# Fetching a part of an embedding lookup row by row from two other DMA issuers

## The chip, the cores and the metric

The kernel runs on one core of a Trainium2 chip. A core has TensorE (PE, matrix products and transposes), VectorE (DVE), ScalarE (ACT), GpSimd (POOL) and SyncE (SP), which run their own instruction streams and meet at semaphores, and 16 DMA engines that move data for all of them. SyncE, ScalarE and GpSimd can issue DMAs. The metric is the device time of one execution in microseconds; before the change it is 11255.83 us, the median of 3 runs (11247.95 to 11278.97).

## What is computed

A recommendation model with attention over 69 id fields. For each of 16384 samples, one label row and 69 field rows of 96 float32 numbers (384 bytes) are looked up in a table of 100001 rows:

```python
u = emb[batch_user]                       # (16384, 69, 96)
ql = emb[batch_label[:, 0]]               # (16384, 96)
q = broadcast(ql over the fields)
z = concatenate([q, u, q - u, q * u], -1)
h = dice(z @ W1 + b1, a1)                 # 384 -> 64
att = (h @ W2 + b2) @ W3 + b3             # -> one number for each field
pre = where(batch_user < 100000, u * att, 0)
pooled = einsum('gf,bfe->bge', window, pre)       # 10 groups of fields
x = concatenate([pooled, ql], -1)                 # 11 * 96
h = dice(bn(x @ Wf1 + bf1)); h = dice(bn(h @ Wf2 + bf2)); out = h @ Wf3 + bf3
```

`dice(x, a)` is `(a * (1 - p) + p) * x` with `p` the sigmoid of the scaled `x`. The lookups are 16384 x 70 rows, 440 MB.

## The kernel before

The batch is cut into 32 blocks of 512 samples. A block has 69 chunks of 512 rows, two of them a "pair" (1104 pairs in all), and a chunk has 4 tiles of 128 rows. A tile is fetched with one indirect DMA, issued by GpSimd, which reads 128 ids from memory:

```python
def gather(table, dst, index):
    nc.gpsimd.indirect_dma_start(out=dst, out_offset=None, in_=table,
        in_offset=bass.IndirectOffsetOnAxis(ap=index, axis=0))          # L257

def head_gather(n):                       # the labels of block n: 4 tiles
    q = bpool.tile([P, NQ, E], F32, tag="q", name=f"q{n}")
    for k in range(NQ):
        gather(emb, q[:, k, :], ids[n][:, NT + k : NT + k + 1])
    return q

def head_turn(n, q):                      # turned to 96 x 512
    pq = ps_x.tile([E, BLK], F32, tag="x", name=f"pq{n}")
    for k in range(NQ):
        nc.tensor.transpose(pq[:, k * P : (k + 1) * P], q[:, k, :], ident)
    nc.vector.tensor_copy(qTs[n % 2][0:E, 0:BLK], pq)
```

A pair is fetched, turned on TensorE, multiplied with the labels on VectorE and copied out of PSUM by ScalarE:

```python
def fetch(i, between=None):
    u = upool.tile([P, 8, E], F32, tag="u", name=f"u{i}")     # upool has 14 buffers
    ...
    for j in range(2):
        n, k = chunk(2 * i + j)
        ptr = ps_tr.tile([E, 512], F32, tag="tr", name=f"ptr{i}_{j}")   # 2 buffers
        for t in range(4):
            gather(rows, u[:, 4 * j + t, :], ids[n][:, 4 * k + t : 4 * k + t + 1])
            nc.tensor.transpose(ptr[:, t * P : (t + 1) * P], u[:, 4 * j + t, :], ident)   # L313
        ...   # VectorE: quT = ptr * labels (L316)
        nc.scalar.copy(uT[j][0:E], ptr)                                 # L325
```

Two steps later `hidden` multiplies with W1 (L338, L342) and forms the dice (ScalarE L344, L345; VectorE L346); then come the attention rows (`attend_rows`, L353) and their turning (`spread`, L370, L375), and eight steps after the fetch `pool` weighs the rows themselves, `acc <- rw, u` (L397). A `u` buffer is free again only after that. Each step `i` of the plan records, in this order:

```python
POOL_LAG = 8
...
at(i, pool_of(i - POOL_LAG)); ...; at(i, tails_of(i - 3)); ...; at(i, hidden_of(i - 2)); at(i, fetch_of(i))
...
for n in range(NBLK):
    first = n * NCH // 2                  # the block's first pair
    if n > 0:
        ...                               # every 4th block: load_ids
        at(first - 14, head_gather of n); at(first - 11, head_turn of n); at(first - 9, head_rows of n)
    ...                                   # the top layers of each block, spread over steps
```

Every engine executes its own instructions in the order in which they are recorded.

Of the kernel before, what the change touches and what calls it, by code (L numbers as in the profile page):

```python
# [32 lines left out]
F32 = mybir.dt.float32  # L33
I32 = mybir.dt.int32
# [4 lines left out]
P = 128  # L39
B, F, E, G = 16384, 69, 96, 10  # L40
ITEM_NUM = 100000
# [5 lines left out]
NBLK = B // BLK  # L47
# [4 lines left out]
NCH = NMAIN + NTAIL  # L52
NQ = BLK // P
NT = NCH * 4
# [5 lines left out]

POOL_LAG = 8

NIDS = 4

EARLY = 20
# [49 lines left out]
def rec_kernel(  # L115
    ctx: ExitStack,
    tc: tile.TileContext,
    idx0: bass.AP,
    idx: bass.AP,
    emb: bass.AP,  # L120
    rows: bass.AP,
    near: bass.AP,
# [3 lines left out]
    nc = tc.nc  # L126
# [4 lines left out]
    tpool = ctx.enter_context(tc.tile_pool(name="tpool", bufs=4))  # L131
    ypool = ctx.enter_context(tc.tile_pool(name="ypool", bufs=6))
    rpool = ctx.enter_context(tc.tile_pool(name="rpool", bufs=2))
    bpool = ctx.enter_context(tc.tile_pool(name="bpool", bufs=2))
    xpool = ctx.enter_context(tc.tile_pool(name="xpool", bufs=1))

    def by_field(ap):

        return ap.rearrange("e (s o) -> e s o", o=1).to_broadcast([ap.shape[0], NS, FM])

    ids = {0: const.tile([P, NCOL], I32, name="ids0")}
    nc.sync.dma_start(out=ids[0], in_=idx0)

    def load_ids(n):

        t = ipool.tile([P, NIDS, NCOL], I32, tag="ids", name=f"ids{n}")
        nc.sync.dma_start(out=t.rearrange("p b n -> p (b n)"), in_=idx[(n - 1) // NIDS])
        for k in range(NIDS):
            ids[n + k] = t[:, k, :]
# [7 lines left out]
    ident = const.tile([P, P], F32, name="ident")  # L157
# [26 lines left out]
    for i in range(2):  # L184
        t = const.tile([E + 1, BLK], F32, name=f"qT{i}")
# [70 lines left out]
    def gather(table, dst, index):  # L256
        nc.gpsimd.indirect_dma_start(  # L257
            out=dst,
            out_offset=None,
            in_=table,  # L260
            in_offset=bass.IndirectOffsetOnAxis(ap=index, axis=0),
        )

    def chunk(c):

        n, k = divmod(c, NCH)
        if n == NBLK - 1 and k >= EARLY:
            k = NMAIN + k - EARLY if k < EARLY + NTAIL else k - NTAIL
        return n, k

    def head_gather(n):

        q = bpool.tile([P, NQ, E], F32, tag="q", name=f"q{n}")
        for k in range(NQ):
            gather(emb, q[:, k, :], ids[n][:, NT + k : NT + k + 1])
        return q

    def head_turn(n, q):
        pq = ps_x.tile([E, BLK], F32, tag="x", name=f"pq{n}")
# [4 lines that stand above are left out]
    def head_rows(n):  # L284

        for h in range(2):
            pc = ps_x.tile([P, NMAIN // 8, H1], F32, tag="x", name=f"pc{n}_{h}")
            for k in range(NMAIN // 8):
                x = (h * NMAIN // 8 + k) * 4 * NS
                nc.tensor.matmul(pc[E:P, k, :], qTs[n % 2][:, x : x + 4 * NS], Cq, start=True, stop=True)  # L290
            nc.scalar.copy(As[n % 2][E:P, h * NMAIN // 8 : (h + 1) * NMAIN // 8, :], pc[E:P])
# [3 lines left out]
    def room(k):  # L295

        v = k % 4 if k < NMAIN else turns.index(min(turns))
        turns[v] += 1
        return uTs[v][turns[v] % len(uTs[v])]

    def fetch(i, between=None):

        u = upool.tile([P, 8, E], F32, tag="u", name=f"u{i}")
        uT = []
        quT = tpool.tile([E, 2, 512], F32, tag="quT", name=f"quT{i}")
        for j in range(2):
            if j == 1 and between:
                between()
            n, k = chunk(2 * i + j)
            ptr = ps_tr.tile([E, 512], F32, tag="tr", name=f"ptr{i}_{j}")  # L310
            for t in range(4):
                gather(rows, u[:, 4 * j + t, :], ids[n][:, 4 * k + t : 4 * k + t + 1])
                nc.tensor.transpose(ptr[:, t * P : (t + 1) * P], u[:, 4 * j + t, :], ident)  # L313
            q = qTs[n % 2][0:E]
            if k < NMAIN:
                nc.vector.tensor_tensor(  # L316
                    quT[:, j, :].rearrange("e (s f) -> e s f", f=FM),
                    ptr.rearrange("e (s f) -> e s f", f=FM),
                    by_field(q[:, k * NS : (k + 1) * NS]),
                    ALU.mult,  # L320
                )
            else:
                nc.vector.tensor_tensor(quT[:, j, :], ptr, q[:, 0:BLK], ALU.mult)
            uT.append(room(k))
            nc.scalar.copy(uT[j][0:E], ptr)  # L325
        return u, uT, quT

    def hidden(i, uT, quT):

# [57 lines left out]
    def pool(i):  # L387

        u, rw = us.pop(i), rws.pop(i)
        todo = [(j, *chunk(2 * i + j)) for j in range(2)]  # L390
        todo = [(j, n, k) for j, n, k in todo if k < NMAIN]
        if not todo:
            return
        pa = ps_acc.tile([E, 2, NS, G], F32, tag="acc", name=f"acc{i}")
        for j, n, k in todo:
            for t in range(4):
                nc.tensor.matmul(  # L397
                    pa[:, j, 2 * t : 2 * t + 2, :].rearrange("e n g -> e (n g)"),
                    u[:, 4 * j + t, :],
                    rw[:, t, j, :],  # L400
                    start=True,
                    stop=True,
                )
        if len(todo) == 2:
            _, n, k = todo[0]
            nc.vector.tensor_copy(  # L406
                pooled[n][:, :, k * NS : (k + 2) * NS].rearrange("e g s -> e s g"),
                pa.rearrange("e j s g -> e (j s) g"),
            )
        else:  # L410
            j, n, k = todo[0]
            nc.vector.tensor_copy(
                pooled[n][:, :, k * NS : (k + 1) * NS].rearrange("e g s -> e s g"), pa[:, j]
            )
# [43 lines left out]
    def store(n):  # L458

        p4 = ps_x.tile([n, P], F32, tag="x", name="p4")  # L460
        nc.tensor.transpose(p4, res[:, 0:n], ident)
        r = ypool.tile([P, 512], F32, tag="y", name="r")[0:n, 0:P]
        nc.vector.tensor_copy(r, p4)
        nc.sync.dma_start(out=out[0 : n * P].rearrange("(m p) o -> m (p o)", p=P), in_=r)
# [9 lines left out]
    pooled, pres, x1s, x2s, qs, us, hs, ys, bands, rws, p1s = ({} for _ in range(11))  # L474

    def top_steps(n, cols):


        def half(h, part):
            if n not in x1s:  # L480
                x1s[n] = xpool.tile([DH, 2, BLK], F32, tag="x1", name=f"x1_{n}")
            p1s[n] = top1(n, cols, h, part, p1s.get(n))

        steps = [lambda h=h, part=part: half(h, part) for h in range(2) for part in range(4)]
        steps.append(lambda: x2s.__setitem__(n, top2(n, cols)))
        if n * BLK + cols.stop < B:
            steps.append(lambda: top3(n, cols, x2s.pop(n)))
        else:
            steps.append(lambda: top3_last(x2s.pop(n)))
        return steps  # L490
# [7 lines left out]
    def pool_of(k):  # L498
        return lambda: pool(k)
# [28 lines left out]
    def at(step, *work):  # L528
        plan.setdefault(step, []).extend(work)
# [25 lines left out]
    for n in range(NBLK):  # L555
        first, end = n * NCH // 2, ((n + 1) * NCH - 1) // 2
        if n > 0:
            if n % NIDS == 1:
                at(first - 20, lambda n=n: load_ids(n))
            at(first - 14, lambda n=n: qs.__setitem__(n, head_gather(n)))  # L560
            at(first - 11, lambda n=n: head_turn(n, qs.pop(n)))
            at(first - 9, lambda n=n: head_rows(n))
        if n < NBLK - 2:
            for s, work in enumerate(top_steps(n, slice(0, BLK))):
                at(end + POOL_LAG + 4 + s, work)
        elif n == NBLK - 2:
            for s, work in enumerate(top_steps(n, slice(0, BLK))):
                at(end + POOL_LAG + s // 2, work)
# [10 lines left out]
    at(d, quarter[2][8], spread_of(c + 6, 2), quarter[2][9], quarter[3][0])  # L579
    at(d, pool_of(c + 6), pool_of(c + 7), lambda: store(B // P - 1), *quarter[3][1:])  # L580

    with tc.manual_schedule():
        qs[0] = head_gather(0)
        head_turn(0, qs.pop(0))
        head_rows(0)
        ones()
        for i in range(NPAIR + 1):
            for work in plan.pop(i, []):
                work()
    assert not plan  # L590


# [60 lines left out]
```

## Time and profile before

| | us |
|---|---|
| timed, median of 3 | 11255.83 |
| span of the profiled execution | 13170.6 |
| GpSimd busy in it | 8455.0 (8966 instructions) |
| TensorE busy in it | 8747.3 |
| ScalarE busy in it | 3167.1 |
| VectorE busy in it | 3029.0 |

The profiled execution is longer than the timed ones, so durations of single instructions and the spacing of undisturbed neighbours are read from it, and the total is taken from the timed runs. In the groups of the profile a row names the source line, engine, operation and operands, then the count, the busy time and the mean of one in ns, and the idle time of the engine just before such instructions with what ended most of it. "issue" means that the engine waited for nothing that the profile shows. A timeline row has the start in us, the duration, and in brackets the idle time before it. "SPq" and "ACTq" are the instruction streams that issue DMAs on SyncE and ScalarE. The DMA queues' part shows 286720 packets of the gathers, which take 16.0% of the 16 DMA engines' time.

### The profile page before, as it was taken

What the parts mean: (1) busy time and instruction counts of PE and PEld (TensorE: products, weight loads), DVE (VectorE), ACT (ScalarE), POOL (GpSimd) and SP (SyncE); (2) the same over time, 40 slices, a digit from 0 to 9 for tenths busy, and PEclk for the clock granted to TensorE, in tenths of its full rate; (3) what the DMA queues carried; (4) which work ended last, traced back from release to release, by engine and by line L of the source; (5) the groups of instructions that cost most, each with busy time, mean ns of one, the idle gap of its engine ahead of it and who ended that gap; (6) DMA issues with size and microseconds to landing.
All of it is one profiled execution on the core that took longest, in us unless ns stands there. A gap on an engine that the chain in (4) does not pass through costs nothing.

```text
span 13170.6 us, 108463 instructions
## 1 busy us (share of the span) xinstructions
PE 8747.3 (66%) x41797; PEld 4554.2 (35%) x41797; DVE 3029.0 (23%) x5325; ACT 3167.1 (24%) x4969; POOL 8455.0 (64%) x8966
## 2 busy tenths in 40 slices
PE   3666666667666676666766667666666666676667
PEld 2333333333333333333333333333333333333334
DVE  2222222222222222222222222222222222222222
ACT  1222222222222222222222222222222222222222
POOL 6666666666666666666666666666666666666664
PEclk6777777777777777767777777777777777777777
DMA  1111111111111111111111111111111111111111
GB/s 40 35 35 34 34 34 37 34 36 34 34 36 34 35 35 35 37 34 34 35 34 37 33 35 34 34 36 35 35 35 33 36 34 35 35 35 35 35 34 22
DMA packets 288946, 454.19 MB, mean 34 GB/s; under 512 B 143538, under 2 KB 143922, under 8 KB 288306
## 3 DMA queue, kind: packets, MB, share of 16 engines
q0 software_dynamic: 286720, 440.98, 16.0%
q8 instruction: 335, 5.49, 0.2%
q1 hardware_dynamic: 1570, 5.04, 0.1%
q14 instruction: 177, 1.45, 0.0%
q10 hardware_dynamic: 144, 1.24, 0.0%
HBM read 446.61 MB, written 0.07 MB: 34 GB/s over the span
## 4 chain that ended last, share of the span: by engine, by line
PE 54%; issue 20%; another core or an unknown queue 16%; POOL 4%; ACT 3%; DVE 3%; DMA 1%; DVEq 0%; POOLq 0%
PE acc L397 11%; PE ptr L313 9%; PE ph L338 9%; PE ph L342 8%; PE p L436 7%; PE prow L353 4%; POOL u L257 3%; PE patt L370 1%; DVE quT L316 1%; PE pa L362 1%; ACT uT L325 1%; ACT y L345 1%; PE ph L335 1%; PE pc L290 1%
## 5 line engine op out<-in xcount | busy, mean ns | idle before, releaser
L257 POOL DMA_INDIRECT u<-in_rows,ids x8832 | 8333.2, 944 | 4552.4 <-issue 2367.4
L397 PE MATMUL acc<-rw,u 128*96 128x20 f32 x16384 | 1922.1, 260 | 1844.3 <-issue 1436.2
L397 PEld LDWEIGHTS acc<-rw,u 128*96 128x96 f32 x16384 | 1911.1, 197 | 2083.9 <-issue 1613.1
L313 PE MATMUL ptr<-ident,u 128*96 128x128 f32 x8832 | 1594.5, 316 | 1395.4 <-issue 1099.1
L325 ACT COPY uT<-ptr 96x512 f32<-96x512 f32 x2208 | 1283.3, 581 | 3091.3 <-DVE quT L316 1905.9
L313 PEld LDWEIGHTS ptr<-ident,u 128*96 128x96 f32 x8832 | 1079.1, 143 | 2732.2 <-issue 2182.7
L344 ACT ACTIVATE y<-ph 128x512 f32<-128x512 f32 x1104 | 659.3, 597 | 5104.0 <-remote 2661.7
L342 PE MATMUL ph<-quT,wn 96*64 96x512 f32 x4416 | 1693.6, 744 | 165.9 <-issue 158.6
L346 DVE TENSOR_TENSOR y<-ph,y 128x512 f32<-128x512 f32 x1104 | 763.5, 692 | 4287.1 <-ACT y L345 2399.0
L338 PE MATMUL ph<-uT,A 128*64 128x512 f32 x4096 | 1631.8, 800 | 145.8 <-issue 142.8
L316 DVE TENSOR_TENSOR quT<-ptr,qT 96x512 f32<-96x512 f32 x2048 | 1337.6, 680 | 1419.3 <-remote 892.2
L406 DVE COPY pooled<-acc 96x160 f32<-96x160 f32 x1008 | 429.6, 426 | 3547.6 <-remote 2121.3
L345 ACT ACTIVATE y<-y,wn,na1c 128x512 f32<-128x512 f32 x1104 | 897.8, 813 | 36.7
L342 PEld LDWEIGHTS ph<-quT,wn 96*64 96x64 f32 x4416 | 449.0, 172 | 1201.8 <-issue 1199.3
L353 PE MATMUL prow<-y,v 128*32 128x512 f32 x2208 | 629.5, 787 | 254.1 <-issue 150.2
L436 PE MATMUL p<-pooled,wf 96*100 96x512 f32 (+1 forms) x1400 | 616.5, 583 | 0.0
L338 PEld LDWEIGHTS ph<-uT,A 128*64 128x64 f32 x4096 | 280.6, 162 | 683.7 <-issue 664.9
L355 ACT COPY row<-prow 128x512 f32<-128x512 f32 (+1 forms) x277 | 161.8, 584 | 1421.8 <-remote 878.8
L370 PE MATMUL patt<-ident,row 128*128 128x128 f32 x1108 | 241.2, 338 | 277.6 <-issue 203.7
L436 PE MATMUL p<-pre,V 96*100 96x512 f32 (+1 forms) x700 | 372.7, 665 | 40.6 <-issue 25.8
L436 PEld LDWEIGHTS p<-pooled,wf 96*100 96x100 f32 x1400 | 233.7, 179 | 291.7 <-issue 291.6
L375 DVE SCALAR_TENSOR_TENSOR rw<-patt,bb,wn 128x320 f32<-128x320 f32 x554 | 273.4, 534 | 142.2 <-remote 64.3
(66 smaller groups left out, 2139.8 us busy)
## 6 DMA issues: line engine op xcount, KB each, us to landing
u<-in_rows,ids POOLq DMA_INDIRECT x8832
ids<-in_idx SPq DMA_DIRECT2D x8, 560.0 KB
q<-in_emb,ids POOLq DMA_INDIRECT x128
wf<-in_far ACTq DMA_DIRECT2D x1, 1209.0 KB
wn<-in_near SPq DMA_DIRECT2D x1, 236.0 KB
ids<-in_idx SPq DMA_DIRECT2D x1, 140.0 KB
out<-r SPq DMA_DIRECT2D x1, 63.5 KB
out<-r SPq DMA_DIRECT2D x1, 0.5 KB
```

Of the source, the lines that this page charges most:

```text
L257: nc.gpsimd.indirect_dma_start(out=dst, out_offset=None, in_=table, in_offset=bass.IndirectOffsetOnAxis(ap=index, axis=0),)
L313: nc.tensor.transpose(ptr[:, t * P : (t + 1) * P], u[:, 4 * j + t, :], ident)
L316: nc.vector.tensor_tensor(quT[:, j, :].rearrange("e (s f) -> e s f", f=FM), ptr.rearrange("e (s f) -> e s f", f=FM), by_field(q[:, k * NS ...
L325: nc.scalar.copy(uT[j][0:E], ptr)
L338: nc.tensor.matmul(p, As[n % 2][:, k // 4, :], uT[j], start=True, stop=False)
L342: nc.tensor.matmul(p, Wp, quT[:, j, :], start=False, stop=True)
L344: nc.scalar.activation(y, ph, AF.Sigmoid, scale=S_DICE)
L345: nc.scalar.activation(y, y, AF.Identity, bias=a1c, scale=na1c)
L346: nc.vector.tensor_mul(y, ph, y)
L353: nc.tensor.matmul(pr[32 * k : 32 * (k + 1), :], v2, ys[b + k], start=True, stop=True)
L397: nc.tensor.matmul(pa[:, j, 2 * t : 2 * t + 2, :].rearrange("e n g -> e (n g)"), u[:, 4 * j + t, :], rw[:, t, j, :], start=True, stop=True,)
L436: nc.tensor.matmul(p1, w[:, h * DH : (h + 1) * DH], x, start=(k == 0), stop=(k == KTOP - 1))
```

## The change

GpSimd issues one indirect DMA for 128 rows. The change takes 7 of the 280 such DMAs of each block but the first away from GpSimd: the four tiles of label rows, and the first tile of the chunks 8, 24 and 40 (the tiles 32, 96 and 160, "solo"). Their rows are fetched one by one, each by a plain DMA of 384 bytes whose source address comes from a register: SyncE issues the first 96 rows of a tile, ScalarE the other 32. The ids come in a new input, `solo`, in the order of use, and are loaded into registers 24 (SyncE) or 8 (ScalarE) at a time. The aim is to relieve GpSimd of issue work.

```diff
+SOLO = [4 * 8, 4 * 24, 4 * 40]
+NROW = NQ + len(SOLO)                    # 7 tiles in a block
+LSP, LACT = 24, 8
+TSP, TACT = 6, 2                         # a turn: six rows by SyncE, two by ScalarE
+TURNS = P // (TSP + TACT)                # 16 turns in a tile, 112 in a block
...
+    def load_solo(n):
+        t = spool.tile([NROW * P // (LSP + LACT), LSP + LACT], I32, tag="sid", name=f"sid{n}")
+        nc.sync.dma_start(out=t, in_=solo[n])
+        sids[n] = t
...
+    def fetch_rows(n, turn):
+        k, m = divmod(turn, TURNS)
+        if turn == 0:
+            qs[n] = bpool.tile([P, NQ, E], F32, tag="q", name=f"q{n}")
+        if k >= NQ and m == 0:
+            solos[n, SOLO[k - NQ]] = spool.tile([P, E], F32, tag=f"solo{k}", name=f"solo{n}_{k}")
+        table, dst = (emb, qs[n][:, k, :]) if k < NQ else (rows, solos[n, SOLO[k - NQ]])
+        part, g = divmod(turn, LSP // TSP)
+        if g == 0:
+            regs[0] = registers(mybir.EngineType.SP, sids[n][part : part + 1, 0:LSP])
+            regs[1] = registers(mybir.EngineType.Activation, sids[n][part : part + 1, LSP:])
+        for e, (dma, num, first) in enumerate([(nc.sync, TSP, 0), (nc.scalar, TACT, TSP * TURNS)]):
+            for i in range(num):
+                p = first + m * num + i
+                dma.dma_start(out=dst[p : p + 1, :], in_=table[bass.ds(regs[e][g * num + i], 1), :])
...
+    def tick(step):
+        while due and due[0][0] <= step:
+            fetch_rows(*due.pop(0)[1:])
...  # in fetch:
-                gather(rows, u[:, 4 * j + t, :], ids[n][:, 4 * k + t : 4 * k + t + 1])
-                nc.tensor.transpose(ptr[:, t * P : (t + 1) * P], u[:, 4 * j + t, :], ident)
+                if (n, 4 * k + t) in solos:
+                    tiles.append(solos.pop((n, 4 * k + t)))
+                else:
+                    tiles.append(u[:, 4 * j + t, :])
+                    gather(rows, tiles[-1], ids[n][:, 4 * k + t : 4 * k + t + 1])
+                nc.tensor.transpose(ptr[:, t * P : (t + 1) * P], tiles[-1], ident)
+            tick(i + (j + 1) / 4)
...  # in the plan:
-            at(first - 14, lambda n=n: qs.__setitem__(n, head_gather(n)))
+            at(first - 33, lambda n=n: load_solo(n))
+            due.extend((first - 32 + (NCH // 2) * x / (NROW * TURNS), n, x) for x in range(NROW * TURNS))
```

The 112 turns of a block's rows are spread evenly over the 34 steps from 32 before the block's first pair on; the turns that are due are recorded after each chunk's transposes (`tick`), and once more at the end of a step. `first_head` keeps the old gathers for the labels of the first block. Tiles of `solo` rows lie in a pool with two buffers each.

More of the change, by code (lines that the diff above doesn't have):

```diff
@@ L119, in rec_kernel @@
     idx: bass.AP,
+    solo: bass.AP,
     emb: bass.AP,
@@ L133, in rec_kernel @@
     rpool = ctx.enter_context(tc.tile_pool(name="rpool", bufs=2))
+    spool = ctx.enter_context(tc.tile_pool(name="spool", bufs=2))
     bpool = ctx.enter_context(tc.tile_pool(name="bpool", bufs=2))
@@ L269, in chunk, with first_head, registers @@
         return n, k
-    def head_gather(n):
-        q = bpool.tile([P, NQ, E], F32, tag="q", name=f"q{n}")
+    def first_head():
+        q = bpool.tile([P, NQ, E], F32, tag="q", name="q0")
         for k in range(NQ):
-            gather(emb, q[:, k, :], ids[n][:, NT + k : NT + k + 1])
+            gather(emb, q[:, k, :], ids[0][:, NT + k : NT + k + 1])
         return q
+    def load_solo(n):
+        t = spool.tile([NROW * P // (LSP + LACT), LSP + LACT], I32, tag="sid", name=f"sid{n}")
+        nc.sync.dma_start(out=t, in_=solo[n])
+        sids[n] = t
+    def registers(engine, index):
+        _, at = nc.values_load_multi_w_load_instructions(
+            index,
+            engines=[engine],
+            min_val=0,
+            max_val=ITEM_NUM,
+            skip_runtime_bounds_check_because="ids are rows of the table",
+        )
+        return list(at)
+    def fetch_rows(n, turn):
[13 more added lines that the diff above has]
+                dma.dma_start(out=dst[p : p + 1, :], in_=table[bass.ds(regs[e][g * num + i], 1), :])
+    regs, sids, solos = [None, None], {}, {}
+    due = []
+    def tick(step):
+        while due and due[0][0] <= step:
+            fetch_rows(*due.pop(0)[1:])
     def head_turn(n, q):
@@ L303, in fetch @@
         u = upool.tile([P, 8, E], F32, tag="u", name=f"u{i}")
-        uT = []
+        uT, tiles = [], []
         quT = tpool.tile([E, 2, 512], F32, tag="quT", name=f"quT{i}")
@@ L325, in fetch @@
             nc.scalar.copy(uT[j][0:E], ptr)
-        return u, uT, quT
+        return tiles, uT, quT
     def hidden(i, uT, quT):
@@ L398, in pool @@
                     pa[:, j, 2 * t : 2 * t + 2, :].rearrange("e n g -> e (n g)"),
-                    u[:, 4 * j + t, :],
+                    u[4 * j + t],
                     rw[:, t, j, :],
@@ L580, in rec_kernel @@
     at(d, pool_of(c + 6), pool_of(c + 7), lambda: store(B // P - 1), *quarter[3][1:])
+    due.sort()
     with tc.manual_schedule():
-        qs[0] = head_gather(0)
-        head_turn(0, qs.pop(0))
+        head_turn(0, first_head())
         head_rows(0)
@@ L589, in rec_kernel @@
                 work()
+            tick(i + 3 / 4)
     assert not plan
@@ L606 @@
     ids = np.concatenate([main, tail, labels], axis=2)
+    solo = np.concatenate([labels] + [main[:, :, k : k + 1] for k in SOLO], axis=2).transpose(0, 2, 1)
+    split = solo[:, :, : TSP * TURNS], solo[:, :, TSP * TURNS :]
+    solo = np.concatenate([split[0].reshape(NBLK, -1, LSP), split[1].reshape(NBLK, -1, LACT)], axis=2)
     groups = np.concatenate([ids[1:], ids[:1]], axis=0).reshape(-1, NIDS, P, NCOL)
@@ L617 @@
         "idx": groups.transpose(0, 2, 1, 3).reshape(-1, P, NIDS * NCOL),
+        "solo": solo,
         "emb": x["emb"],
```

## The prediction

> **What bounds the kernel now.** I read the page's first two parts, then the groups, then single rows of the GpSimd timeline, because a busy share says nothing about pitch. The head of the page:
>
> ```profile
> span 13170.6 us, 108463 instructions
> PE 8747.3 (66%) x41797; PEld 4554.2 (35%) x41797; DVE 3029.0 (23%) x5325; ACT 3167.1 (24%) x4969; POOL 8455.0 (64%) x8966
> ```
>
> [...]No engine is over 66% busy, so the page alone does not name the bound. The costliest groups (line, engine, operation; count; busy us, mean ns; idle before):
>
> ```profile
> L257 POOL DMA_INDIRECT u<-in_rows,ids x8832 | 8333.2, 944 | 4552.4 <-issue 2367.4
> L397 PE MATMUL acc<-rw,u 128*96 128x20 f32 x16384 | 1922.1, 260 | 1844.3 <-issue 1436.2
> L325 ACT COPY uT<-ptr 96x512 f32<-96x512 f32 x2208 | 1283.3, 581 | 3091.3 <-DVE quT L316 1905.9
> ```
>
> GpSimd issues one gather of 128 rows after another. Its timeline (start, duration, idle before) gives the pitch:
>
> ```profile
> 6200.46 0.94 POOL L257 DMA_INDIRECT u<-in_rows,ids  x1 [0.30 <-issue]
> 6201.71 0.94 POOL L257 DMA_INDIRECT u<-in_rows,ids  x1 [0.30 <-DMA u<-in_rows,ids]
> ...
> 6206.70 0.94 POOL L257 DMA_INDIRECT u<-in_rows,ids  x1 [0.31 <-issue]
> 6207.95 0.94 POOL L257 DMA_INDIRECT u<-in_rows,ids  x1 [0.30 <-issue]
> 6216.18 0.94 POOL L257 DMA_INDIRECT u<-in_rows,ids  x1 [7.29 <-PE prow L353]
> ```
>
> From 6159.27 to 6207.95 us there are 39 steps in 48.68 us: 1.248 us each. There are 8832 + 128 = 8960 gathers; 8960 x 1.248 = 11182 us. The timed 11256 leaves 74 us, which the start (the first gather is at 7.04 us) and the tail fill. So unprofiled, GpSimd issues without a gap and **is the bound**. The waits of the profiled run, like the last row above, follow disturbances of up to 43 us that the profile puts on TensorE, and the timed runs cannot contain many of them.
>
> Two more views size the change. The only rows that SyncE's queue has:
>
> ```profile
> 0.75 0.40 SPq L142 DMA_DIRECT2D ids<-in_idx  x1
> 1.21 0.44 SPq L153 DMA_DIRECT2D wn<-in_near  x1
> ...
> 13168.46 0.26 SPq L472 DMA_DIRECT2D out<-r  x1
> ```
>
> A 128-row load holds SyncE 0.40 to 0.44 us, with about 0.05 us to the next; the single-row store 0.26 us. And TensorE working off a backlog, with all operands ready, shows how fast it can catch up:
>
> ```profile
> 6246.98 1.46 PE L397 MATMUL acc<-rw,u 128*96 128x20 f32 x16
> 6248.37 1.08 PE L338 MATMUL ph<-uT,A 128*64 128x512 f32 x4
> 6249.28 1.03 PE L342 MATMUL ph<-quT,wn 96*64 96x512 f32 x4
> 6250.24 1.08 PE L313 MATMUL ptr<-ident,u 128*96 128x128 f32 x8
> 6251.16 1.46 PE L397 MATMUL acc<-rw,u 128*96 128x20 f32 x16
> ```
>
> From acc to acc, one pair of chunks in 4.2 us; with the rows, tails and top layers of other steps, I take 5.5 to 6 us. GpSimd needs 8 x 1.248 = 9.98 us for a pair.
>
> [...]The trace has the label gather that starts at 11.07 us for 0.94 us, and TensorE using it at 13.54, 1.5 us after its issue ended. [...]DMA engines are 16% busy with the gathers.
>
> **The change, part by part.**
>
> 1. *Removed from GpSimd*: 4 label gathers and 3 tile gathers in 31 blocks, 217 of 8960. 217 x 1.248 = 271 us. With nothing else, 11256 - 271 = **10985 us** (2.4% less). This is the floor of what the change can reach, as GpSimd still issues 8743.
>
> 2. *Added to SyncE*: 31 x 672 = 20832 row DMAs, each after one register instruction (the id times the row's bytes), and 868 register loads of 24 ids. A row: 0.26 + 0.05 gap + 0.04 to 0.09 for the register instruction (my guess from that gap), 0.35 to 0.40 us. A block: 672 x 0.37 + 28 x 0.9 = 274 us, against GpSimd's 273 x 1.248 = 341. By its sum SyncE isn't the bound.
>
> 3. *Added to ScalarE*: 6944 row DMAs and 868 loads of 8 ids, per block 224 x 0.37 + 28 x 0.7 = 102 us beside 3167 / 32 = 99 us of work. 201 of 341: not the bound either.
>
> 4. *What moves: the lock-step.* In the order of the built program each row DMA on either engine first waits for one of eight shared completion semaphores, whose last user was the eighth DMA before it in one common order. So neither engine can be more than eight rows past a row that the other hasn't issued. That order isn't the even "six by SyncE, two by ScalarE" of the source. In every block it lets ScalarE run ahead: when ScalarE has issued its share of turn 71 (of 112), SyncE may only have come to turn 36; then 175 SyncE rows stand in a row, and likewise some 153 (from turn 86 to 111) before ScalarE's first turn of the next block. Both runs sit where the others must wait. The labels' last rows are of turn 63, and the TensorE transposes of the labels come right after ScalarE's turn 71: SyncE has (64 - 36) x 6, about 166 rows, to go, and TensorE stands. At the block's end the next ids are loaded by SyncE behind all its rows, and ScalarE's register load stands until they land.
>
>  First stall: 166 x 0.37 + 7 x 0.9 + 2 to land + 3 = 73 us. GpSimd may run ahead: 14 buffers of a pair each, released 8 steps later (POOL_LAG), are 6 pairs, 6 x 9.88 = 59 us. It loses 73 - 59, about 14 us.
>  Between the stalls lie 40 turns, 12.3 pairs. At 5.8 us a pair TensorE takes 71 us, in which GpSimd does 7.2; its lead is back to 1.1 pairs, the room to 4.9 pairs, 48 us.
>  Second stall: 153 x 0.37 + 6 x 0.9 + 3 = 65 us, less about 10 us in which TensorE still has work: 55 - 48 = 7 us lost. The 22 pairs after it restore all the room.
>  So 14 + 7 = 21 us in a block, less some overlap; I take 18: 31 x 18 = 560 us.
>
> Sum: 11256 - 271 + 560 = about **11545 us**.
>
> **The rivals.**
>
> *GpSimd stays the bound throughout.* If a row costs 0.30 us, the same sums give stalls of 61 and 44 us, about the room of 59 and 48, and the time is near 10985. For it: busy sums leave all engines slack, and the split between two issuers leaves each time to spare. Against it: the issue alone is 0.26 in the trace.
>
> *SyncE becomes the bound.* At 0.45 us a row its block is 672 x 0.45 + 25 = 327 us, nearly GpSimd's 341, but the stalls grow to 86 and 67: 27 + 19 lost in each block, about 12400 us. A row whose address is in a register may well cost that; no such row is in the trace.
>
> *The single-row transfers are slow to land.* All rows share eight semaphores; [...]Over 3 us to land, landing sets the pace and the second rival's times follow.
>
> *ScalarE's own work is delayed by its DMA waits.* For it: it executes in order, and TensorE's transposes need its copies (L325). Against it: outside the two stretches it is the engine ahead. I give it under 100 us.
>
> **Range and chances.** The time turns on SyncE's row cost: 0.30 gives 10985, 0.35 about 11400, 0.37 11545, 0.45 about 12400. I choose 11550 and 10980 to 12450. Under 11031 (faster by 2%) needs a row below about 0.31 us or more room than counted: 0.25. Within 2%, up to 11481, is 0.31 to 0.36 us: 0.23. Beyond: 0.52.
>
> **What would show it.** GpSimd's pitch stays 1.248 us with 8743 gathers (step 1). SyncE's row-to-row spacing inside a long run is 0.35 to 0.40 us (step 2). ScalarE stays near 60% (step 3). TensorE waits some 60 to 75 us at the label transposes once a block, and GpSimd waits 10 to 20 us for TensorE soon after (step 4). I am wrong if TensorE hardly waits there, if SyncE's spacing is far from 0.37, or if GpSimd has gaps spread over the whole block.

## The result and the profile after

The changed kernel takes 12040.08 us, median of 4 runs (12023.08 to 12049.83), against 11254.27 for the kernel before on the same chip: ratio 1.0692, 95% interval 1.0672 to 1.0712. It is 786 us slower, where the prediction had 294 slower. The direction and the mechanism were right; the predicted size was less than half of the measured one.

The head of the page of the changed kernel (its line numbers are 9 to 55 higher than before: L257 is now L266, L313 L367, L325 L380, L397 L452; L331 are the label transposes, L318 the row DMAs, L294 the register loads):

```profile
span 12039.7 us, 194245 instructions
PE 6921.0 (57%) x41797; PEld 3865.6 (32%) x41797; DVE 2943.2 (24%) x5325; ACT 3146.3 (26%) x4969; POOL 8252.4 (69%) x8749
```

There are 85782 more instructions, nearly all of them issue work of SyncE and ScalarE, and no engine has more busy time than before. The loss must be waiting. The groups (line, engine, operation, count; busy us, mean ns; idle before, and what ended it):

```profile
L266 POOL DMA_INDIRECT u<-in_rows,ids x8739 | 8247.6, 944 | 3719.7 <-issue 2508.7
L380 ACT COPY uT<-ptr 96x512 f32<-96x512 f32 x2208 | 1271.7, 581 | 4394.0 <-DMA q<-in_emb 2562.9
L331 PE MATMUL pq<-ident,q 128*96 128x128 f32 x128 | 46.2, 371 | 2577.9 <-DMA q<-in_emb 2573.2
```

One gather still takes 944 ns. But the 128 label transposes, 46 us of work, have 2578 us of TensorE idle before them: 83 us in each of 31 blocks, waiting for label rows. TensorE's waits name a second stall, in which it stands for ScalarE's copies, and GpSimd's waits name the damage (waiter, what it waited for: total us, times, longest):

```profile
PE pq L331 <- DMA q<-in_emb: 2573.2, 65, 47.1
PE ptr L367 <- ACT uT L380: 2288.1, 330, 73.5
```

```profile
POOL u L266 <- PE acc L452: 1045.8, 82, 39.5
```

GpSimd waits 1046 us for TensorE to release `u` buffers. Adding up its steps longer than 1.30 us in the trace, less the usual 1.248, gives 1057 us; 11256 - 271 + 1057 = 12042. The whole result is accounted for.

One block in time, from TensorE's timeline (only its rows with a long wait, and the transposes that precede one):

```profile
5741.67 1.09 PE L367 MATMUL ptr<-ident,u 128*96 128x128 f32 x4 [68.65 <-ACT uT L380]
5876.82 0.68 PE L331 MATMUL pq<-ident,q 128*96 128x128 f32 x2
5915.19 0.42 PE L331 MATMUL pq<-ident,q 128*96 128x128 f32 x1 [37.68 <-DMA q<-in_emb]
5962.42 0.42 PE L331 MATMUL pq<-ident,q 128*96 128x128 f32 x1 [46.81 <-DMA q<-in_emb]
6114.76 1.94 PE L367 MATMUL ptr<-ident,u 128*96 128x128 f32 x8 [70.17 <-ACT uT L380]
```

At 5876.82 the first two of the four label tiles are there; the third comes 38 us later, the fourth 47 us after that. TensorE keeps the recorded order: GpSimd gathers up to 48 tiles ahead in this stall, and TensorE works 1.4 of its 86 us. From 5882 to 5971 us ScalarE issues no row, and SyncE issues alone:

```profile
5881.51 0.64 ACTq L318 DMA_DIRECT2D solo<-in_rows  x2
...
5971.19 1.67 ACTq L318 DMA_DIRECT2D solo<-in_rows  x4
```

```profile
5866.75 94.48 SPq L318 DMA_DIRECT2D q<-in_emb  x192
```

When ScalarE has issued the last row of its turn 71 here (5881.9), SyncE has issued 221 rows of the block, not quite 37 turns; before ScalarE's next row it issues 177 more. The trace also shows the lock itself: every row DMA of both engines names one of eight semaphores (100, 102 to 104, 115 to 118; 3471 to 3473 of the 27776 rows each), and the two sequences fit into one common order that takes these eight in turn. In that order 176 to 179 and 149 to 161 SyncE rows stand in a row in every block but the first (175 and 153 in the prediction). Outside these runs it is SyncE that is held back, waiting for earlier row DMAs for 1465 us in all:

```profile
SPq L318 <- DMA q<-in_emb: 1013.1, 847, 18.8
SPq L318 <- DMA solo<-in_rows: 451.7, 395, 11.0
```

The same block cut at these points (stretch: length; busy us of PE, PEld, DVE, ACT and POOL; granted clock; DMA share, GB/s):

```profile
5742.00:5877.00 135.00, 128.60 (x745) 70.58 (x743) 51.26 (x92) 58.63 (x92) 102.04 (x109) 0.93 0.20 42
5877.00:5963.00 86.00, 1.38 (x7) 0.89 (x7) 2.01 (x4) 2.57 (x4) 41.51 (x44) 0.51 0.13 27
5963.00:6045.00 82.00, 77.84 (x539) 44.62 (x538) 36.59 (x67) 35.16 (x56) 60.25 (x64) 0.95 0.20 40
6045.00:6115.00 70.00, 0.24 (x2) 0.23 (x3) 0.00 (x0) 0.63 (x2) 52.92 (x57) 0.51 0.19 41
```

TensorE works at 95% in the first and third stretch and stands in the second and fourth. GpSimd carries on in the second until its buffers are full (44 gathers, 55 us of 86), and stops:

```profile
5965.55 0.94 POOL L266 DMA_INDIRECT u<-in_rows,ids  x1 [33.63 <-PE acc L452]
```

What SyncE's instructions cost (durations in ns, min/median/max):

```profile
L318 SPq DMA_DIRECT2D q<-in_emb x11904: 224/225/306, 9.1 to 11589.4; - x199
```

```profile
L294 SPq TENSOR_LOAD <-sid x868: 1582/1714/1894, 7.3 to 11740.6; - x174
L294 ACTq TENSOR_LOAD <-sid x868: 717/738/1012, 38.7 to 11671.5; - x174
```

A row DMA holds SyncE 225 ns, and with its register instructions the median step from row to row is 408 ns. A load of 24 registers takes 1714 ns; the step across it is about 2.17 us, so it adds some 1.75.

### The profile page after: what moved, and what is told of

It reads as the page before. It is cut to its first block, busy times and chain, and to the rows that moved or that the text cites. A ratio compares the mean times of both kernels' runs of the same rounds, so it can differ in the third digit from the quotient of the medians.

```text
span 12039.7 us, 194245 instructions
## 1 busy us (share of the span) xinstructions
PE 6921.0 (57%) x41797; PEld 3865.6 (32%) x41797; DVE 2943.2 (24%) x5325; ACT 3146.3 (26%) x4969; POOL 8252.4 (69%) x8749
## 4 chain that ended last, share of the span: by engine, by line
PE 34%; SPq 30%; issue 16%; ACT 7%; ACTq 4%; DMA 4%; POOL 3%; DVE 2%; DVEq 0%; POOLq 0%
SPq L318 24%; PE p L491 7%; PE acc L452 7%; SPq L294 5%; PE ph L393 5%; PE ph L397 5%; PE ptr L367 5%; ACTq L318 4%; POOL u L266 3%; ACT y L400 2%; PE prow L408 2%; ACT uT L380 2%; ACT y L399 2%; DMA solo<-in_rows 2%; DVE quT L371 2%
## 5 line engine op out<-in xcount | busy, mean ns | idle before, releaser
L266 POOL DMA_INDIRECT u<-in_rows,ids x8739 | 8247.6, 944 | 3719.7 <-issue 2508.7
L367 PE MATMUL ptr<-ident,u 128*96 128x128 f32 x8739 | 1346.5, 290 | 2414.3 <-ACT uT L380 2278.8
L380 ACT COPY uT<-ptr 96x512 f32<-96x512 f32 x2208 | 1271.7, 581 | 4394.0 <-DMA q<-in_emb 2562.9
L367 PEld LDWEIGHTS ptr<-ident,u 128*96 128x96 f32 x8739 | 944.3, 131 | 3487.5 <-ACT uT L380 2720.2
L452 PEld LDWEIGHTS acc<-rw,u 128*96 128x96 f32 x16198 | 1634.2, 177 | 139.1 <-issue 126.8
L452 PE MATMUL acc<-rw,u 128*96 128x20 f32 x16198 | 1620.0, 245 | 4.9 <-DVE pooled L461 4.3
L331 PE MATMUL pq<-ident,q 128*96 128x128 f32 x128 | 46.2, 371 | 2577.9 <-DMA q<-in_emb 2573.2
L397 PE MATMUL ph<-quT,wn 96*64 96x512 f32 x4416 | 1286.3, 649 | 0.0
L393 PE MATMUL ph<-uT,A 128*64 128x512 f32 x4096 | 1269.2, 691 | 0.6 <-ACT uT L380 0.6
L331 PEld LDWEIGHTS pq<-ident,q 128*96 128x96 f32 x128 | 18.3, 144 | 2600.9 <-issue 1669.3
L397 PEld LDWEIGHTS ph<-quT,wn 96*64 96x64 f32 x4416 | 358.6, 152 | 744.1 <-issue 743.9
L408 PE MATMUL prow<-y,v 128*32 128x512 f32 x2208 | 407.8, 704 | 31.5 <-DVE y L401 20.7
L393 PEld LDWEIGHTS ph<-uT,A 128*64 128x64 f32 x4096 | 222.0, 146 | 339.7 <-issue 322.6
```

The source lines that it names most:

```text
L367: nc.tensor.transpose(ptr[:, t * P : (t + 1) * P], tiles[-1], ident)
L393: nc.tensor.matmul(p, As[n % 2][:, k // 4, :], uT[j], start=True, stop=False)
L397: nc.tensor.matmul(p, Wp, quT[:, j, :], start=False, stop=True)
L452: nc.tensor.matmul(pa[:, j, 2 * t : 2 * t + 2, :].rearrange("e n g -> e (n g)"), u[4 * j + t], rw[:, t, j, :], start=True, stop=True,)
```

## The experiments

All ratios are to the kernel before, run on the same chip in the same session, with 95% intervals.

### ScalarE without rows

```diff
-        for e, (dma, num, first) in enumerate([(nc.sync, TSP, 0), (nc.scalar, TACT, TSP * TURNS)]):
+        if m == 0:
+            nc.sync.dma_start(out=dst[96:128, :], in_=table[0:32, :])   # rows nobody asked for
+        for i in range(TSP): ...                                          # SyncE's rows as before
```

The load of ScalarE's registers is left out with its rows.

> As the changed kernel, but ScalarE issues no row: rows 96 to 127 of each of the 7 tiles come with one DMA of 32 neighbouring table rows from SyncE (so those rows are not the ones asked for). SyncE's 96 single rows per tile and its register loads stay. Lock-step theory (SyncE is held back by rows that ScalarE hasn't issued yet, and then has to catch up alone while TensorE stands): SyncE runs free, the 83 us waits at the label transposes and the 68 us waits at the block's first turn vanish, and GpSimd is the bound again: 10985 to 11080 us. Rate theory (SyncE with 672 x 0.408 + 28 x 1.75 + waits is simply too slow and sets the 373 us block): SyncE's work is unchanged, so 12000 us or a little more. ScalarE theory (its own copies come late because it issues rows): also near 11000.

Measured: 10984.88 us, ratio 0.9758 (0.9742 to 0.9774). TensorE's longest total wait is now the gathers, as it should be in a kernel that GpSimd bounds, no wait for labels is left, and SyncE's row DMAs wait 3 us in all instead of 1465. GpSimd waits for released buffers 3 us in all:

```profile
PE ptr L367 <- DMA u<-in_rows,ids: 1966.4, 2343, 2.4
PE patt L425 <- DVE pre L418: 15.4, 17, 1.0
```

```profile
POOL u L266 <- PE acc L452: 3.0, 10, 0.3
```

SyncE still issues all its 20832 single rows and 868 loads. So neither their number, nor their landing, nor SyncE's pace alone costs the time. The prediction's floor, 10985 us, is met. What is gone is ScalarE's part, and that can act in two ways: as a lock on SyncE, or as a burden on ScalarE.

### Half and half

```diff
-LSP, LACT = 24, 8
-TSP, TACT = 6, 2
+LSP, LACT = 16, 16
+TSP, TACT = 4, 4
```

> As the changed kernel, but a turn is four rows by SyncE and four by ScalarE instead of six and two. In the built order the two engines' rows now alternate evenly; no run of one engine's rows is longer than 26. Lock-step theory: no stall, GpSimd is the bound, 10985 to 11100 us. ScalarE theory (rows delay its copies and activations): ScalarE has twice the rows, 448 x 0.40 + 28 x 1.2 + 99 of own work = 312 us in a block, so slower than the changed kernel, over 12100. Rate theory: SyncE has a third less to do, so GpSimd-bound as well.

Measured: 10985.70 us, ratio 0.9761 (0.9745 to 0.9777). ScalarE issues twice as many rows as in the change, and the two stalls are gone: it isn't the burden. TensorE's waits are short, and most are for gathers:

```profile
PE ptr L367 <- DMA u<-in_rows,ids: 1733.5, 2109, 2.5
PE ptr L367 <- ACT uT L380: 262.6, 202, 4.3
```

The eight shared semaphores are still there; what differs is the order of the rows, and that SyncE has fewer of them. The order is not as even as I expected. No run of SyncE rows is longer than 33, but ScalarE is now the one behind: in 25 of the 31 blocks it has 64 to 74 rows left when SyncE has issued its own, and 532 in the last block. SyncE then stands until the next ids can be loaded (L290):

```profile
SPq L290 <- DMA solo<-in_rows: 1149.1, 26, 52.4
```

This costs nothing: nobody waits for SyncE meanwhile. In the changed kernel the long runs did harm because ScalarE, which they stop, has its copies in the same stream, and because the rows in them were overdue. This kernel leaves nothing out, and is faster than the kernel before and the changed one.

### The rows 12 steps earlier

```diff
-            at(first - 33, lambda n=n: load_solo(n))
-            due.extend((first - 32 + ..., n, x) for x in range(NROW * TURNS))
+            at(max(first - 45, 1), lambda n=n: load_solo(n))
+            due.extend((max(first - 44 + ..., 2), n, x) for x in range(NROW * TURNS))
```

> As the changed kernel, but a block's ids are loaded and its rows are recorded 12 steps earlier. Nothing else: as many rows, loads and transposes. In the built order the run of about 175 SyncE rows before the label transposes is gone, and there is one run of about 321 rows before ScalarE's first turn of each block. Lock-step theory: no wait at the label transposes, one stall of 321 x 0.408 + 13 x 1.75 + 5 = 159 us a block, less a room of about 65 us: 94 us lost, about 13900 us. Rate theory or a plain deadline theory (labels come too late): the labels have 120 us more, so 12040 or better.

Measured: 13650.12 us, ratio 1.2123 (1.2103 to 1.2143). More time to fetch, and the kernel is 1610 us slower than the change. TensorE's wait has moved from the labels to ScalarE, where the built order has its run of 321 SyncE rows:

```profile
PE ptr L367 <- ACT uT L380: 3014.5, 210, 131.2
...
PE pq L331 <- DMA q<-in_emb: 604.3, 35, 29.7
```

This is the sharpest test: a late deadline or a slow SyncE can't make an earlier start cost time, and the order can. SyncE's long run takes 158 to 161 us, as summed. TensorE stands for 129 of them in the median, as it first waits some 19 us for labels, which I had expected to vanish, and then has work for a while. Because of that first wait GpSimd is already 18 tiles ahead when the long stall begins; it loses 90 us in a block (94 expected).

### Two u buffers fewer

```diff
-    upool = ctx.enter_context(tc.tile_pool(name="upool", bufs=14))
+    upool = ctx.enter_context(tc.tile_pool(name="upool", bufs=12))
```

> As the changed kernel with 12 instead of 14 u buffers; the order of all rows is the same. Stall-beyond-room theory: both stalls stay (83 and 68 us), GpSimd's room shrinks by two pairs, 20 us, at each: 32 + 20 lost at the first, about 4 + 20 at the second, 76 us in a block, about 13300 us. Rate theory (SyncE's pace sets the block): GpSimd's look-ahead doesn't matter, 12040.

Measured: 12680.75 us, ratio 1.1264 (1.1245 to 1.1282), 641 us slower than the change; I expected 1260. GpSimd's wait grows with the same stalls:

```profile
POOL u L266 <- PE acc L452: 1689.3, 98, 48.6
```

In the medians of the trace, the label stall costs 46 of 80 us instead of 35 of 84, so the room is 34 us instead of 50. How far GpSimd gets can be counted: its gathers begun, less the tiles that TensorE has transposed. It stops exactly 32 tiles ahead, four pairs, at every label stall, and exactly 48, six pairs, in the changed kernel. The room shrinks by less than those 20 us because it also starts less far ahead, 3 tiles instead of 5. The second stall, 63 us, costs 8 instead of 0 in the median. Together 55 us are lost in a block where I had 76. A stall thus costs what exceeds GpSimd's look-ahead.

### Registers loaded once in a block

```diff
-        if g == 0:
+        if turn == 0:
             regs[0] = registers(...); regs[1] = registers(...)
```

All turns of a block then use the same ids, so most rows aren't the ones asked for.

> As the changed kernel, but each engine loads registers only once in a block and uses the same 24 or 8 ids for every turn (so most rows are not the ones asked for); 27 of 28 register loads a block on each engine are left out, all rows stay. In the built order the runs of SyncE rows alone are shorter too (about 137 before the label transposes, about 122 before the next block). Lock-step theory with a 1.71 us register load as the term I sized wrong: the wait at the label transposes falls from 83 to about 128 x 0.408 + 5 = 57 us, 7 us over the room of 50, the second to 55 us, inside its room: 10985 + 31 x 7 = about 11200 us. If the loads hardly matter: 12000.

Measured: 10988.81 us, ratio 0.9761 (0.9745 to 0.9778). The label stall is 51 us in the median, in two pieces of some 12 and 39, and the second 38:

```profile
PE pq L331 <- DMA solo<-in_rows: 908.0, 23, 41.3
PE pq L331 <- DMA q<-in_emb: 673.1, 50, 39.5
```

GpSimd gets at most 46 tiles ahead in the label stall, just short of its 48, and loses nothing. So the loads, as a duration and through the order that was built with them, are what lifts the stalls over the room. The run of rows is also shorter here (136 to 144 for 176 to 179), so this run doesn't size the duration of a load by itself.

### Labels only, six and two

```diff
-SOLO = [4 * 8, 4 * 24, 4 * 40]
+SOLO = []
```

The rows are recorded 46 steps ahead of the block.

> As the changed kernel with the labels' four tiles alone fetched row by row (the three solo tiles are gathered by GpSimd again), six rows by SyncE and two by ScalarE, recorded over the same number of steps, 46 steps before the block. The lock-step remains: the built order has one run of about 113 SyncE rows per block, before ScalarE's first turn. Stall-beyond-room theory: 113 x 0.408 + 5 x 1.75 + 5 = 60 us, less than the room of 65, so nothing is lost: 11256 - 124 x 1.248 = 11101 us. If any lock-step costs time by itself: 11300 or more.

Measured: 11099.24 us, ratio 0.9861 (0.9844 to 0.9877). 11101 was expected. The lock-step is there and TensorE stands 33 to 45 us once a block (55 in the first), for nothing lost: a stall inside the room is free.

### Eight tiles, five and three

```diff
-SOLO = [4 * 8, 4 * 24, 4 * 40]
-TSP, TACT = 6, 2
+SOLO = [4 * 8, 4 * 20, 4 * 32, 4 * 44]
+TSP, TACT = 5, 3                          # LSP, LACT = 20, 12
```

> Eight tiles (labels and four solo tiles), five rows by SyncE and three by ScalarE in a turn. GpSimd's floor is 11256 - 248 x 1.248 = 10946 us. The built order has one run of about 139 SyncE rows before ScalarE's first turn of each block: 139 x 0.408 + 7 x 1.5 + 5 = 72 us against a room of about 65. Stall-beyond-room theory: 5 to 10 us lost in a block, 11100 to 11250 us. If only the stall at the label transposes mattered: 10946.

Measured: 10953.67 us, ratio 0.9731 (0.9715 to 0.9747). The floor of this version is 10946. TensorE stands for 57 us in the median, 65.7 at most, and GpSimd doesn't notice:

```profile
PE ptr L367 <- ACT uT L380: 2393.4, 559, 65.7
```

```profile
POOL u L266 <- PE acc L452: 11.3, 37, 0.3
```

The stall was 15 us shorter than my sum and fell inside the room that I had put at 65: SyncE's run of 140 rows takes 68 us, but TensorE has work for the first of them. TensorE has as much waiting for ScalarE here (2393 us) as in the change (2288), and the time is at its floor: the total of a wait says nothing, its length against the look-ahead does. This version leaves nothing out either, and none that was run is faster.

### Eight tiles, nine and seven

```diff
-LSP, LACT = 20, 12
-TSP, TACT = 5, 3
+LSP, LACT = 18, 14
+TSP, TACT = 9, 7
```

> Eight tiles, nine rows by SyncE and seven by ScalarE in a turn; the built order alternates, no run over 23. SyncE has 576 x 0.408 + 32 x 1.7 = 289 us of issue in a block, ScalarE 448 x 0.393 + 32 x 1.4 + 102 = 323 us, GpSimd 272 x 1.248 = 339 us. Lock-step theory: GpSimd-bound, 10946 us (0.36% below the half-and-half kernel). If ScalarE at 95% delays its copies: over 11050.

Measured: 11414.65 us, ratio 1.0157 (1.012 to 1.0194): a miss. There are no long stalls; TensorE waits for ScalarE in 862 pieces of up to 8.8 us. The cause stands in the register loads:

```profile
L294 SPq TENSOR_LOAD <-sid x992: 1550/1688/1913, 7.4 to 11037.8; - x199
L294 ACTq TENSOR_LOAD <-sid x992: 3169/3312/3582, 38.9 to 11033.6; - x199
```

14 registers on ScalarE take 3.31 us, twice as long as 18 on SyncE. The ids of ScalarE begin at byte 72 of a row here. Two runs ask whether it is the address or the count: the same kernel with two unused ids in between (byte 80), and the half-and-half kernel with two unused ids (byte 72 for 64).

```diff
-        t = spool.tile([..., LSP + LACT], I32, tag="sid", name=f"sid{n}")
+        t = spool.tile([..., LSP + LACT + 2], I32, tag="sid", name=f"sid{n}")
...
-            regs[1] = registers(mybir.EngineType.Activation, sids[n][part : part + 1, LSP:])
+            regs[1] = registers(mybir.EngineType.Activation, sids[n][part : part + 1, LSP + 2 :])
```

> As the nine-seven kernel, whose ScalarE loads of 14 registers from byte 72 of a row took 3.31 us each, with two unused ids between SyncE's 18 and ScalarE's 14, so that ScalarE's start at byte 80. If the start address made them slow: 14 registers in about 1.2 us (12 took 1.06, 16 took 1.27), ScalarE's issue in a block falls from about 390 to 323 us and GpSimd is the bound: 10946 to 10985 us. If the count of 14 made them slow: 3.3 us and 11410 us as before.

> As the half-and-half kernel with two unused ids between SyncE's 16 and ScalarE's 16, so that ScalarE's loads start at byte 72 instead of 64. If the start address is the cause: 16 registers take 3.3 us or more instead of 1.27, 28 x 2.1 = 59 us more of ScalarE in each block, which has some 30 us to spare: 11000 to 11300 us. If not: 10986 us.

Measured: nine and seven padded, 10971.37 us, ratio 0.9731 (0.9714 to 0.9747), level with five and three; half and half from byte 72, 11138.28 us, ratio 0.9888 (0.9854 to 0.9922). The loads of ScalarE, padded first, then from byte 72:

```profile
L294 ACTq TENSOR_LOAD <-sid x992: 1384/1447/1733, 38.9 to 10586.6; - x199
```

```profile
L294 ACTq TENSOR_LOAD <-sid x868: 3584/3755/3963, 38.7 to 10770.6; - x174
```

The address alone makes 14 registers 1.45 or 3.31 us, and 16 registers 1.27 or 3.76.

## Why the prediction was right, and where it was wrong

*The bound before, and step 1*: right. GpSimd's pitch stays 1.249 us with 8743 gathers, and three kernels without harmful stalls lie at 10985 to 10989, where step 1 put the floor at 10985.

*Step 2, SyncE's cost*: a row steps at 0.408 us where I took 0.37 from a range up to 0.40; a load of 24 registers adds 1.75 us where I took 0.9, half as much. The 0.9, and the 0.7 for 8 registers in step 3, were estimates without a measurement: the trace of the kernel before has no register load. Together 672 x 0.408 + 28 x 1.75 = 323 us a block, not 274.

*Step 3, ScalarE's cost*: right in that it isn't the bound; with a row step of 0.40 us and a load of 8 registers that adds 0.9 (in the trace 0.398 to 0.406 us from row to row and 1.28 to 1.31 across a load where ScalarE isn't held back), 224 x 0.40 + 28 x 0.9 + 98 of its own work are about 213 us in a block.

*Step 4, the lock-step*: the mechanism and the order are as stated, and **the loss at the first stall was mis-sized**: 14 us in the prediction, 35 in the median of the trace. Two terms make the difference.

- The stall is 84 us where the sum had 73. 166 x 0.408 + 7 x 1.75 + 5 = 85 with the measured row and load, so the count was right and the two durations of step 2 were short. The 5 (2 to land, 3 more) is still the prediction's estimate; in the trace TensorE goes on 1.25 us in the median (0.99 to 1.79) after the last label row it waits for was issued.
- The room is 50 us, not 59. The limit was right: GpSimd stops exactly 48 tiles, six pairs, ahead. But the sum let it start level with TensorE and go on the moment TensorE does. It is 2 to 8 tiles ahead when TensorE begins to stand (5 in the median, 6 us), and its next gather comes 3.1 us after the last label tile, when `acc` has freed a buffer. 48 x 1.249 - 6 - 3 leaves 51 us.

The second stall is 69 us long, was expected to cost 7 us, and costs 0 in the median, 2 in the mean. Here the room is larger than counted: GpSimd gets up to 69 tiles ahead. A `u` buffer isn't always held until eight steps after its fetch. `pool` returns at once for a pair that has only chunks of the last five of a block, so its buffer is free after its transposes. Two such pairs are among the buffers in use at this place, and 48 + 16 tiles and the rest of a pair fit the count. (The prediction's 4.9 pairs of room should also read 12.3 - 7.2 = 5.1.)

"The 22 pairs after it restore all the room" holds, but barely. TensorE does 21 pairs between the two stalls in 135 us at 95% busy, 6.4 us a pair where I took 5.8, and brings GpSimd's lead from 64 tiles down to 5; in the half-and-half kernel, which has no stalls, the lead at the labels is 2. In the whole run TensorE waits only 128 us for gathers, against 1734 there: 86 + 70 us of standing and 217 us of work fill the block's 373 us.

I then took 18 for a sum of 21 "for overlap", the wrong way: the trace has 1057 / 31 = 34 us a block.

*The rivals*: "GpSimd stays the bound throughout" is what the other orders give. "SyncE becomes the bound" at 0.45 us a row had stalls of 86 and 67 us, close to the 84 and 69 measured, but by luck: the row takes 0.408, and the register loads are the rest. Slow landing and ScalarE's own delay played no part, by the first two experiments.

What isn't shown: why the built order lets ScalarE run ahead with six and two, and SyncE with four and four. I read the order from the built programs, and the semaphores in the traces agree with it; what made it is open. It is also open whether six and two in an even order would reach the floor; no run has both.

## What to carry to other kernels

When two engines issue DMAs that share a set of semaphores, eight here, look at the built order of their DMAs: 176 to 179 rows of SyncE's in a row were a stretch in which ScalarE issued none (89 us in the block shown) and TensorE stood for 84 us. If others depend on such a stretch, compare it with the look-ahead of the engine that bounds the kernel, counting only as much look-ahead as the others have had time to rebuild. Stalls of 33 to 45 us (labels only), 51 us (registers loaded once) and 57 us (five and three) cost nothing here; of 84 us against a room of 50, 35 were lost. A busy sum that leaves each engine slack (323 and about 213 of 341 us here) did not show this.

## What was not expected of the hardware

- A register load from memory took longer with more registers, and far longer from one address. From a row's bytes 0, 64, 80 or 96: 8 registers 0.74 us and 24 1.71 (the change), 12 1.06 (five and three), 16 1.26 on SyncE and 1.27 on ScalarE (half and half); from 12 to 24 that is about 0.055 us a register. Two counts stand above this line: 14 took 1.45 (nine and seven padded), more than 16, and 18 took 1.69 (nine and seven), nearly as much as 24. From byte 72, 14 took 3.31 (nine and seven) and 16 took 3.76 (half and half from byte 72), about 0.22 us for each of the two registers between. Only these sizes and addresses were run, and none of the runs shows what makes a load slow.
- A row DMA with its address in a register held SyncE 225 ns (its next instruction starts 0.05 us after) and ScalarE 235 ns, less than the 260 ns of the plain single-row store on SyncE in the kernel before. The rest of SyncE's 408 ns step is register instructions (37 and 29 ns) and the time between instructions.
- TensorE, after standing 69 and 86 us, was granted 0.93 and 0.95 of its clock in the next stretch of the block shown above, and 0.51 in the two stretches in which it stood; the mean of a run was 0.73 to 0.79.
